# A planned GNN stack: batch-norm aggregation moved to GpSimd, a doubled recurrent state, and 67 single-pass state products

## The chip, the cores and the metric
The kernel runs on one core of one Trainium2 chip. The metric is the device time of one execution in microseconds (us), the median of several runs.

## The reference
The input `x` holds 32 batches of 512 tokens by 128 features, and `adj` is one 512 x 512 matrix that all batches share. Four layers follow, and each adds its result to `x`. Each starts from `h = relu(layernorm(x))`.

```python
# layer 0: graph convolution
A = adj + I;  d = A.sum(-1) ** -0.5
x = x + ((d[:, None] * A * d[None, :]) @ h) @ W.T + b
# layer 1: gated recurrent network, five steps (in_matrix and out_matrix are both adj)
m = adj @ h;  av = concat(m, m);  u3 = h @ u3_w.T
z = sigmoid(av @ w3_w.T + u3);  r = sigmoid(av @ w4_w.T + u3)
hv = tanh(av @ w5_w.T + (r * h) @ u5_w.T)
h = (1 - z) * h + z * hv
# layers 2 and 3: graph attention, softmax over the neighbours of each token
```
Everything is float32.

## The kernel before
All work is put into a list of operations by `op(engine, cost, due, emit, r, w, delay)` (class `Plan`). Each operation has an engine, a planned duration, a due time, a function that emits its instructions, and the buffers that it reads and writes. `Plan.run` simulates the five engines with these costs and delays, picks for each free engine the ready operation that is due first, and takes a buffer from its pool when an operation first needs one. The order found in this way is the order in which each engine's instructions are issued; each engine then executes in that order. `NUDGES` is a list of seeds that shift due times at random in stretches of the plan. So a changed cost, delay, buffer number or operation changes the order everywhere. Up to `LANES` = 6 batches are in the recurrent layer at once, one begun about every five planning slots.

A 128 x 512 product with float32 accuracy is made in one of two ways. One is a plain FP32 matmul (`weigh`, L807). The other takes three single passes (`one_pass`, L810; L691 for products with the adjacency matrix): `operands` (L664, L665, L667) makes three rounded tiles `upper`, `lower` and `across` with one ACT and two DVE operations; the passes of `upper` and `lower` add into a PSUM bank, ACT scales the bank by SPLIT + 1 (`rescale`, L673), and the pass of `across` is added.

`ggnn` normalizes a batch, brings it into feature order in `hT`, and calls `step` five times. A step has a product with `adj` (`in_three`), the gate r, the gate z in the same bank, and the candidate. In the steps of `STATE_GATES` the product with u3 takes three passes (`parts` of `by_m`), in the others an FP32 matmul. After r the bank is scaled back by 1/(SPLIT + 1), because z adds two unscaled passes first. Three DVE operations (L858, L859, L861) make the new state. `shuttle` carries the state back to token order by a DVE transpose (L642) into `sq` and five DMAs.

`norm_relu` makes the layernorm: `norm_stats` has four `bn_stats` (L553) and four `bn_aggr` (L557) on DVE. GpSimd then takes four operations on 128 x 4: add eps (L565), the power -0.5 (L566), the negated mean (L567), and its product with `rstd` (L570). Four ACT operations (L572) apply scale, offset and relu. `gcn` calls it for layer 0, `ggnn` for layer 1, and `gat` for the attention layers of batches 0 to 27 (the last four use `center_relu`). `add_onto` (L636) adds a result to `x` by a DMA that GpSimd issues, so these transfers and the small operations share one queue.

Of the kernel before, what the change touches and what calls it, by code (L numbers as in the profile page):

```python
# [24 lines left out]
FAR0 = 2  # L25
IDLE_FROM = 1342
# [3 lines left out]
STATE_GATES = {(b, s) for b in range(2, 32) for s in (2, 3) if s == 2 or b % 2}  # L30

NUDGES = (
    647971, 907480, 641022, 815328, 59938, 583104, 493449, 610727, 19299, 304899, 627144, 635903, 69303, 408061,
    213735, 192787, 7302, 58637, 834115, 963636, 6410, 705202, 955061, 53160, 882452, 878871, 458378, 231573,
    440371, 124696, 831158, 659333, 156550, 375431, 144007, 229366, 92171, 712320, 383813, 271697, 742240,
    798210, 397175, 163443, 123863, 724213, 516264, 896604, 122936, 743614, 457019, 570185, 62661, 920948,
    442263, 711198, 25011, 31858, 120261, 992683, 84663, 643357, 45247, 844390, 187975, 852865, 391757, 659128,
    736213, 659734, 397346, 484557, 410316, 685524, 527983, 521839, 433865, 543542, 868384, 394072, 205808,
    803310, 720274, 491124, 788541, 970038, 794737, 126558, 819621, 549318, 737826, 829243, 433351, 616176,
    868933, 314847, 688289, 939737, 907635, 853367, 672087, 953482, 982700, 636640, 260426, 745621, 974814,  # L40
    394689, 394423, 913904, 563868, 809734, 586161, 212429, 918084, 35227, 367565, 563487, 894884, 927872,
    820562, 407961, 31584, 797859, 266733, 239356, 49239, 168566, 825959, 690462, 633213, 766471, 952403,
    408935, 497281, 589831, 985192, 831666, 253050, 326020, 481827, 642272, 794393, 288155, 810682, 987219,
    726505, 745342, 441796, 26158, 800211, 187528, 795534, 149175, 951249, 42293, 197549, 962585, 253163,
    193842, 380099, 269941, 798210, 328761, 3598, 288464, 573452, 270841, 123133, 696935, 118976, 888464,
    549179, 731891, 706853, 313783, 900776, 668175, 816491, 294510, 923659, 444695, 534341, 679525, 202474,
    575303, 728118, 586387, 249556, 511121, 99992, 373622, 338542, 275589, 302881, 192606, 296189, 6121, 900716,
    93206, 158600, 419776, 382555, 10260, 855575, 704212, 698851, 696052, 457683, 55138, 404164, 139732, 866775,
    158170, 353170, 522421, 782841, 883529, 937879, 284896, 89904, 707913, 653847, 899032, 941515, 846706,
    471855, 178908, 722182, 666466, 211415, 810021, 295037, 269035, 402549, 983916, 571726, 473540, 395183,  # L50
    828707, 575084, 168839, 283291, 285134, 921509, 310987, 390552, 988218, 707221, 197452, 843224, 366926,
    884427, 545850, 986879, 832460, 861905, 777944, 317120, 973125, 261515, 931720, 503469, 106085, 519250,
    799711, 171717, 223192, 984270, 900296, 444443, 363172, 878758, 209540, 540746, 177829, 80204, 926590,
    322517, 646401, 549673, 224793, 442843, 438276, 448009, 366213, 419202, 112410, 62545, 971608, 549811,
    277513, 626388, 256930, 747343, 895280, 67763, 895530, 719737, 906641, 169362, 565633, 657856, 621526,
    269556, 28511, 630184, 65022, 38094, 940486, 350670, 532843, 24899, 947205, 540231, 223974, 479634, 329335,
    298114, 146538, 491725, 308524,
# [264 lines left out]
def gnn_stack(ctx: ExitStack, tc: tile.TileContext, a: dict, out: bass.AP):  # L322
# [13 lines left out]
    def flat(t):  # L336
# [8 lines left out]
        "sq": tiles(4, [P, Q, W * C], "sq"),  # L345
# [7 lines left out]
        "r": tiles(8, TOKENS, "r"),  # L353
# [13 lines left out]
        "ve": tiles(4, SMALL, "ve"),  # L367
        "rstd": tiles(8, SMALL, "rstd"),
# [28 lines left out]
    mhalf, eps, minus1 = (fixed(SMALL, k) for k in ("mhalf", "eps", "minus1"))  # L397
    warm = Val("r")
    op("POOL", 0.8, -1000, lambda: make_identity(nc, ident.t), w=[ident])
    for v, to in ((mhalf, -0.5), (eps, EPS), (minus1, -1.0)):  # L400
        op("POOL", 0.1, -999, lambda v=v, to=to: nc.gpsimd.memset(v.t, to), w=[v])
# [11 lines left out]
    for b in range(B):  # L413
        v = Val("x", C)
        op("SP", 0.5, -1002 if b == 0 else max(-995 + b, STEPS * b - 20) if b >= 8 else -995 + b,
           lambda v=v, b=b: nc.sync.dma_start(v.t, x[b].rearrange("(c p) d -> p c d", p=P)), w=[v], delay=(3.75, 5.2, 4.5, 5)[b] if b < 4 else 3)
        xs.append(v)
# [95 lines left out]
    def one(v):  # L513
        return [(v, 0, ident)]

    w0T = transposed(-11.7, one(w0), then=turned)
    gates = transposed((-9.5, -700, -700, -15.8), one(raw["u3"]), halves("w4"), halves("w3") + halves("w4", minus), halves("w5"), then=turned)
# [10 lines left out]
    u5T = transposed(-15.2, one(raw["u5"]), then=turned, by=0.5)  # L528
# [32 lines left out]
    def norm_relu(b, y, due, times=None):  # L561

        xb, off, rstd = xs[b], Val("off"), Val("rstd")
        mv = norm_stats(b, due)
        op("POOL", 0.5, due, lambda: nc.gpsimd.tensor_tensor(rstd.t, mv.t[:, :, 1], eps.t, ALU.add), r=[mv, eps], w=[rstd])  # L565
        op("POOL", 1.15, due, lambda: nc.gpsimd.tensor_tensor(rstd.t, rstd.t, mhalf.t, ALU.pow), r=[mhalf], w=[rstd])  # L566
        op("POOL", 0.42, due, lambda: nc.gpsimd.tensor_tensor(off.t, mv.t[:, :, 0], minus1.t, ALU.mult), r=[mv, minus1], w=[off])  # L567
        if times:
            op("DVE", 0.1, due, lambda: nc.vector.tensor_mul(rstd.t, rstd.t, times.t), r=[times], w=[rstd])
        op("POOL", 0.42, due, lambda: nc.gpsimd.tensor_tensor(off.t, off.t, rstd.t, ALU.mult), r=[rstd], w=[off], delay=2.6)  # L570
        for c in range(C):
            op("ACT", 0.385, due, lambda c=c: nc.scalar.activation(  # L572
                chunk(y, c), xb.t[:, c, :].rearrange("p (k j) -> p k j", k=Q) if y.kind == "h" else xb.t[:, c, :], AF.Relu, bias=off.t[:, c:c + 1], scale=rstd.t[:, c:c + 1]),
               r=[xb[c], off, rstd], w=[y[c * len(y.writers) // C]])
# [60 lines left out]
    def add_onto(x, what, reads, due):  # L635
        op("POOL", 1.0, due, lambda: nc.gpsimd.dma_start(x.t, what(), accum_op=ALU.add), r=reads, w=[x], delay=5.5)  # L636
# [147 lines left out]
    def ggnn(b, due):  # L784
        lane, h, hT = Val("lane"), Val("h" if b >= FAR0 else "y", C), Val("hT", Q)
        op("SP", 0.0, due - 3, lambda: None, r=[xs[b]], w=[lane], delay=0)
        op("SP", 0.0, due - 3, lambda: None, r=[lane], w=[h], delay=0)
        norm_relu(b, h, due - 2)
        if b >= FAR0:
            shuttle_first(h, hT, due - 2.5, due - 3)  # L790
        else:
            p = to_features(h, due - 2, hT)
            op("ACT", COPY, due - 2, lambda hT=hT: nc.scalar.copy(flat(hT.t), flat(p.t)), r=[p], w=[hT])
        for s in range(STEPS):
            now = due + LANES * s
            split = (b, s) not in WHOLE_GATES
            m = in_three(h, factors["adj"], now, split)
            if b == 4 and s == 0:
                op("SP", 0.0, now, lambda: None, r=[m[0] if split else m], w=[third], delay=0)
            h, hT = step(b, s, m, hT, now, lane)  # L800

    def step(b, s, m, hT, due, lane):
# [9 lines left out]
        def by_m(p, i, at, start, more=None, parts=None):  # L812
# [24 lines left out]
            op("PE", 2 * len(sums) * MR, at, first_two, r=[*of_gates[:2], *(v for _, three in sums for v in three[:2])], w=[p])  # L837
            rescale(p, at - 5)
            op("PE", len(sums) * MR + (MM if more else 0), at, third_one, r=[of_gates[2], *(three[2] for _, three in sums), *rest], w=[p])
# [9 lines left out]
        if split:  # L849
            rescale(gate, due - 5, 1 / (SPLIT + 1))  # L850
        by_m(gate, 2, due + 0.3, False)
        op("ACT", A, due - 5, lambda: nc.scalar.activation(flat(z.t), flat(gate.t), AF.Tanh, bias=gate_b["w3"].t, scale=0.5),
           r=[gate, gate_b["w3"]], w=[z])
        hv, new = Val("r"), Val("hT")
# [3 lines left out]
        op("DVE", V, due - 5, lambda: nc.vector.tensor_sub(flat(hv.t), flat(hv.t), flat(hT.t)), r=[hT], w=[hv])  # L858
        op("DVE", V, due - 5, lambda: nc.vector.scalar_tensor_tensor(flat(hv.t), flat(z.t), 1.0, flat(hv.t), op0=ALU.add, op1=ALU.mult),  # L859
           r=[z], w=[hv])  # L860
        op("DVE", V, due - 5, lambda: nc.vector.scalar_tensor_tensor(flat(new.t), flat(hv.t), 0.5, flat(hT.t), op0=ALU.mult, op1=ALU.add),  # L861
           r=[hv, hT], w=[new])
# [3 lines left out]
        if not EARLY <= due < STEPS * B:  # L866
            p = to_features(new, due + 2, *([] if last else [h]))
            if last:
                op("DVE", V, due + 2, lambda: nc.vector.tensor_add(flat(x.t), flat(x.t), flat(p.t)), r=[p, lane], w=[x])
# [5 lines left out]
        if last:  # L875
            mine = Val("y", 2)
            op("ACT", COPY, due + 2, lambda: nc.scalar.copy(
                mine.t.rearrange("p c (k j) -> p c k j", k=Q), h.t.rearrange("p k (c j) -> p c k j", c=C)), r=[h], w=[mine])
# [217 lines left out]
```

## Time and profile before

| what | us |
|---|---|
| median of 3 runs (1497.68 to 1499.28) | 1498.44 |
| the profiled execution | 1498.66 |
| its span, first to last instruction | 1496.7 |
| TensorE matmuls busy | 1486.3 |
| VectorE busy | 1408.1 |
| ScalarE busy | 1332.4 |
| GpSimd busy | 445.6 |

The span is shorter than the execution's time by 2.0 us, which lie around it. Engines run beside each other. PE is TensorE, PEld its weight loads, DVE VectorE, ACT ScalarE, POOL GpSimd, SP the queue that issues most DMAs. L with a number is a line of the kernel. A busy time is a union of instruction spans; successive instructions of one engine overlap a little in the trace, so distances between starts are also used.

### The profile page before, as it was taken

To read this page: it belongs to the slowest core of one execution; us is meant where nothing else is said; L and a number is where in the kernel's file an instruction comes from. 1 tells how busy PE (TensorE), PEld (TensorE's weight loads), DVE (VectorE), ACT (ScalarE), POOL (GpSimd) and SP (SyncE) were. 2 spreads that over 40 slices of the span, in tenths; PEclk is the share of its full clock that TensorE was granted. 3 is DMA by queue.
4 is the path that set the end of the run, shared out by engine and by line. 5 is a ranking of instruction groups with operands and counts; after the bars stand their busy time and mean duration, and the time that the engine had idled before them with its cause. 6 is when DMAs were issued, how large, how long until landed. Compare 5 with 4: busy or idle time off the path is not lost.

```text
span 1496.7 us, 25563 instructions
## 1 busy us (share of the span) xinstructions
PE 1486.3 (99%) x7464; PEld 1168.4 (78%) x7464; DVE 1408.1 (94%) x3323; ACT 1332.4 (89%) x2994; POOL 445.6 (30%) x636
## 2 busy tenths in 40 slices
PE   9999999999999999999999999999999999999999
PEld 7777777777777778777778777777777787777888
DVE  8989998999998998999999999999899999999898
ACT  6988998998989899989899989899889889989875
POOL 5411322222254223332323322333332214202321
PEclk9999999999999999999999999999999999999999
DMA  3345555645767567666665667666566565653233
GB/s 106 60 100 144 101 127 117 164 120 127 173 132 154 135 149 162 141 142 144 145 153 130 149 142 163 141 148 139 129 149 158 134 152 117 152 147 75 71 73 78
DMA packets 307499, 196.09 MB, mean 131 GB/s; under 512 B 87872, under 2 KB 259232, under 8 KB 307360
## 3 DMA queue, kind: packets, MB, share of 16 engines
q1 hardware_dynamic: 276160, 157.24, 40.8%
q0 software_dynamic: 30912, 36.71, 16.1%
q8 instruction: 59, 0.97, 0.3%
q14 instruction: 80, 0.66, 0.2%
q10 hardware_dynamic: 288, 0.52, 0.1%
HBM read 87.30 MB, written 70.37 MB: 105 GB/s over the span
## 4 chain that ended last, share of the span: by engine, by line
PE 54%; DVE 5%; ACT 4%; DMA 2%; issue 1%; SPq 1%; POOL 0%; DVEq 0%; ACTq 0%; POOLq 0%
PE bank L691 18%; PE bank L810 14%; PE bank L807 9%; PE bank L1001 8%; PE bank L932 3%; PE bank L987 1%; ACT bank L673 1%; DVE e L975 1%; PE bank L769 1%; DVE lower L665 1%; DVE across L667 1%; DMA far<-sq 1%; ACT upper L664 1%; DMA adjT<-y 1%; DVE sq L642 0%
## 5 line engine op out<-in xcount | busy, mean ns | idle before, releaser
L673 ACT ACTIVATE bank<-bank 128x512 f32<-128x512 f32 x820 | 466.4, 599 | 48.8 <-PE bank L691 35.4
L667 DVE SCALAR_TENSOR_TENSOR across<-lower,upper 128x512 fp32r<-128x512 f32 x391 | 260.2, 675 | 2.4 <-DVE lower L665 0.5
L810 PE MATMUL bank<-upper,gates 128*128 128x512 f32 x519 | 240.2, 463 | 0.1
L1001 PEld LDWEIGHTS bank<-h_gat,e 128*128 128x128 f32 x1792 | 220.3, 191 | 20.9 <-issue 12.0
L810 PE MATMUL bank<-across,gates 128*128 128x512 f32 x519 | 227.5, 466 | 1.0 <-ACT bank L673 0.9
L1001 PE MATMUL bank<-h_gat,e 128*128 128x129 f32 x1792 | 222.8, 275 | 0.0
L810 PE MATMUL bank<-lower,gates 128*128 128x512 f32 x519 | 204.9, 395 | 0.3 <-DVE lower L665 0.2
L691 PE MATMUL bank<-adj,across 128*128 128x512 f32 x640 | 188.3, 419 | 0.1
L691 PE MATMUL bank<-adj,upper 128*128 128x512 f32 x640 | 187.3, 414 | 0.0
L691 PE MATMUL bank<-adj,lower 128*128 128x512 f32 x640 | 175.4, 396 | 0.0
L636 POOL DMA_DIRECT2D x<-y x80 | 73.7, 928 | 315.4 <-ACT y L778 82.2
L565 POOL TENSOR_TENSOR rstd<-mv,eps 128x4 f32<-128x4 f32 x119 | 55.9, 470 | 371.4 <-DVE mv L557 363.0
L807 PE MATMUL bank<-r,wT 128*128 128x512 f32 x320 | 163.6, 593 | 2.0 <-DVE r L847 2.0
L975 DVE SCALAR_TENSOR_TENSOR e<-row,h_gat,maskT 128x512 f32<-128x512 f32 x224 | 156.9, 738 | 0.0
L566 POOL TENSOR_TENSOR rstd<-rstd,mhalf 128x4 f32<-128x4 f32 x119 | 150.4, 1264 | 1.5
L691 PEld LDWEIGHTS bank<-adj,across 128*128 128x128 f32 x640 | 117.5, 188 | 42.4 <-issue 12.5
L691 PEld LDWEIGHTS bank<-adj,upper 128*128 128x128 f32 x640 | 118.2, 188 | 37.0 <-issue 12.2
L691 PEld LDWEIGHTS bank<-adj,lower 128*128 128x128 f32 x640 | 120.4, 188 | 28.6 <-DVE lower L665 0.4
L810 PEld LDWEIGHTS bank<-across,gates 128*128 128x128 f32 x519 | 96.6, 188 | 49.1 <-ACT bank L673 20.3
L810 PEld LDWEIGHTS bank<-upper,gates 128*128 128x128 f32 x519 | 97.9, 189 | 37.9 <-issue 13.2
L845 ACT ACTIVATE r<-bank,gate_bw 128x512 f32<-128x512 f32 x160 | 111.1, 696 | 15.7 <-PE bank L807 15.4
L810 PEld LDWEIGHTS bank<-lower,gates 128*128 128x128 f32 x519 | 98.0, 189 | 32.7 <-issue 14.6
(153 smaller groups left out, 3073.1 us busy)
## 6 DMA issues: line engine op xcount, KB each, us to landing
far<-sq SPq DMA_DIRECT2D x936, 64.0 KB
h<-far SPq DMA_DIRECT2D x148, 256.0 KB
x<-y POOLq DMA_DIRECT2D x80, 256.0 KB, 4.3
sq<-far SPq DMA_DIRECT2D x56, 256.0 KB
row<-line SPq DMA_DIRECT2D x56, 256.0 KB
adjT<-y POOLq DMA_DIRECT2D x32, 256.0 KB, 4.2
hT<-far SPq DMA_DIRECT2D x120, 64.0 KB
x<-in_x_dram SPq DMA_DIRECT2D x24, 256.0 KB
```

The costliest lines, as they stand in the source:

```text
L565: op("POOL", 0.5, due, lambda: nc.gpsimd.tensor_tensor(rstd.t, mv.t[:, :, 1], eps.t, ALU.add), r=[mv, eps], w=[rstd])
L566: op("POOL", 1.15, due, lambda: nc.gpsimd.tensor_tensor(rstd.t, rstd.t, mhalf.t, ALU.pow), r=[mhalf], w=[rstd])
L636: op("POOL", 1.0, due, lambda: nc.gpsimd.dma_start(x.t, what(), accum_op=ALU.add), r=reads, w=[x], delay=5.5)
L667: op("DVE", V, due - 5, lambda: nc.vector.scalar_tensor_tensor(flat(across.t), flat(lower.t).bitcast(F32), -SPLIT, flat(upper.t).bitcast(F ...
L673: op("ACT", COPY, due, lambda: nc.scalar.mul(flat(p.t), flat(p.t), by), w=[p])
L691: nc.tensor.matmul(flat(p.t), left.t[:, c, :], right.t[:, c, :], start=first and c == 0, stop=c == C - 1, skip_group_check=True)
L807: nc.tensor.matmul(flat(p.t), (of or gates).t[:, i, :], flat(moving.t), start=start, stop=True, skip_group_check=True)
L810: nc.tensor.matmul(flat(p.t), of.t[:, i, :], flat(moving.t), start=start, stop=True, skip_group_check=True)
L845: op("ACT", A, due - 5, lambda: nc.scalar.activation(flat(r.t), flat(gate.t), AF.Tanh, bias=gate_b["w4"].t, scale=0.5), r=[gate, gate_b["w ...
L932: nc.tensor.matmul(qt()[:, c, :D + 3], gT.t[:, 2 * a + c, :], w_aug[l].t, start=True, stop=True)
L975: op("DVE", 0.661, due + 3, lambda j=j: nc.vector.scalar_tensor_tensor(e.t[:, j, :], matrix(row), h.t[:, j, D + 1:D + 2], mask.t[:, j, :], ...
L1001: nc.tensor.matmul(pt()[:, c, :D + 1], e.t[:, j, i * P:(i + 1) * P], h.t[:, j, :D + 1], start=(j == 0), stop=(j == C - 1))
```

## The change
Five things are changed.

1. The state is kept doubled: the layernorm of layer 1 multiplies `rstd` by two, the transposed gate weights are halved and those of u5 quartered, and the last step's result is halved. The new state is made from `kept = (z - 1) * hT`, which does not read the candidate, and two more DVE operations.
2. The z product adds its `across` pass first (`back=True`), on the scaled bank; the bank is then scaled back once and the other two passes follow. The tanh of z takes the factor SPLIT + 1 in its scale. The separate scaling between r and z is gone.
3. From batch 4 (`AGGR`) on, `norm_relu` has no `bn_aggr`. GpSimd combines the two halves' means and variances of `bn_stats` itself, in ten operations on 128 x 4 (one of them on 128 x 8).
4. `STATE_GATES` holds 67 steps instead of 45.
5. The planned delays of the loads of `x` (3 to 8) and of `add_onto` (5.5 to 7) are longer, `sq` has three buffers instead of four, `r` nine instead of eight, and the seeds are others.

```diff
+AGGR = 4
-STATE_GATES = {(b, s) for b in range(2, 32) for s in (2, 3) if s == 2 or b % 2}
+STATE_GATES = {(b, s) for b in range(2, 32) for s in (1, 2, 3) if s > 1 or b % 4 == 1}
...
-        "sq": tiles(4, [P, Q, W * C], "sq"),
+        "sq": tiles(3, [P, Q, W * C], "sq"),
...
-        "r": tiles(8, TOKENS, "r"),
+        "r": tiles(9, TOKENS, "r"),
...
-w=[v], delay=(3.75, 5.2, 4.5, 5)[b] if b < 4 else 3)
+w=[v], delay=(3.75, 5.2, 4.5, 5)[b] if b < 4 else 8)
...
+        if b < AGGR:
...
+        else:
+            st, both, apart = Val("st", C), Val("both"), Val("apart")
+            scale = root2 if state else root
+            for c in range(C):
+                op("DVE", 0.196, due, lambda c=c: nc.vector.bn_stats(st.t[:, c, :], xb.t[:, c, :]), r=[xb[c]], w=[st[c]])
+            pool(0.42, lambda: apart.t, lambda: st.t[:, :, 1], lambda: st.t[:, :, 4], ALU.subtract, [st], [apart])
+            pool(0.42, lambda: both.t, lambda: st.t[:, :, 1:3], lambda: st.t[:, :, 4:6], ALU.add, [st], [both])
+            pool(0.42, lambda: apart.t, lambda: apart.t, lambda: apart.t, ALU.mult, [], [apart])
+            pool(0.42, lambda: apart.t, lambda: apart.t, lambda: c32.t, ALU.mult, [c32], [apart])
+            pool(0.42, lambda: apart.t, lambda: apart.t, lambda: eps128.t, ALU.add, [eps128], [apart])
+            pool(0.42, lambda: rstd.t, lambda: apart.t, lambda: both.t[:, :, 1], ALU.add, [apart, both], [rstd])
+            pool(1.15, lambda: rstd.t, lambda: rstd.t, lambda: mhalf.t, ALU.pow, [mhalf], [rstd])
+            pool(0.42, lambda: rstd.t, lambda: rstd.t, lambda: scale.t, ALU.mult, [scale], [rstd])
+            pool(0.42, lambda: off.t, lambda: both.t[:, :, 0], lambda: nhalf.t, ALU.mult, [both, nhalf], [off])
...
-        op("POOL", 1.0, due, lambda: nc.gpsimd.dma_start(x.t, what(), accum_op=ALU.add), r=reads, w=[x], delay=5.5)
+        op("POOL", 1.0, due, lambda: nc.gpsimd.dma_start(x.t, what(), accum_op=ALU.add), r=reads, w=[x], delay=7)
...
+            if back:
+                op("PE", MR, at, third_one, r=one_of, w=[p])
+                rescale(p, at - 5, 1 / (SPLIT + 1))
+                op("PE", 2 * MR, at, first_two, r=two_of, w=[p])
+                return
...
-        if split:
-            rescale(gate, due - 5, 1 / (SPLIT + 1))
-        by_m(gate, 2, due + 0.3, False)
-        op("ACT", A, due - 5, lambda: nc.scalar.activation(flat(z.t), flat(gate.t), AF.Tanh, bias=gate_b["w3"].t, scale=0.5),
+        by_m(gate, 2, due + 0.3, False, back=True)
+        op("ACT", A, due - 5, lambda: nc.scalar.activation(
+            flat(z.t), flat(gate.t), AF.Tanh, bias=gate_b["w3"].t, scale=0.5 * (SPLIT + 1) if split else 0.5),
...
-        hv, new = Val("r"), Val("hT")
+        hv, kept, new = Val("r"), Val("r"), Val("hT")
+        op("DVE", V, due - 5, lambda: nc.vector.scalar_tensor_tensor(flat(kept.t), flat(z.t), -1.0, flat(hT.t), op0=ALU.add, op1=ALU.mult),
+           r=[z, hT], w=[kept])
...
-        op("DVE", V, due - 5, lambda: nc.vector.tensor_sub(flat(hv.t), flat(hv.t), flat(hT.t)), r=[hT], w=[hv])
...
-        op("DVE", V, due - 5, lambda: nc.vector.scalar_tensor_tensor(flat(new.t), flat(hv.t), 0.5, flat(hT.t), op0=ALU.mult, op1=ALU.add),
-           r=[hv, hT], w=[new])
+        op("DVE", V, due - 5, lambda: nc.vector.scalar_tensor_tensor(flat(new.t), flat(kept.t), -0.5, flat(hv.t), op0=ALU.mult, op1=ALU.add),
+           r=[hv, kept], w=[new])
```
The cut parts are the other norm branch (as before, with the product by two where the state is normed), the halved weights and results, six constants, and the seeds.

## Prediction
> **What bounds the kernel now.** I read the page's busy times and granted clock first, then the waits of TensorE, then the groups for the price of each operation, then the timeline for the true pace of the matmuls.
>
> ```profile
> PE 1486.3 (99%) x7464; PEld 1168.4 (78%) x7464; DVE 1408.1 (94%) x3323; ACT 1332.4 (89%) x2994; POOL 445.6 (30%) x636
> PEclk9999999999999999999999999999999999999999
> ```
> ```profile
> PE bank L807 <- DVE r L847: 2.0, 1, 2.0
> PE bank L409 <- DVE r L402: 1.1, 1, 1.1
> PE bank L810 <- ACT bank L673: 0.9, 3, 0.4
> ```
> TensorE is busy throughout at the full clock, and its three longest sorts of wait come to 4 us in 1496.7. A busy TensorE may still hide bubbles, so the pace of starts is the better measure:
>
> ```profile
> 800.26 0.80 PE L810 MATMUL bank<-across,gates 128*128 128x512 f32 x1
> 800.89 1.02 PE L807 MATMUL bank<-hT,wT 128*128 128x512 f32 x2
> 801.35 0.79 PE L810 MATMUL bank<-across,gates 128*128 128x512 f32 x1
> ...
> 809.23 0.39 PE L810 MATMUL bank<-upper,gates 128*128 128x512 f32 x1
> 809.46 0.40 PE L810 MATMUL bank<-lower,gates 128*128 128x512 f32 x1
> 809.70 0.40 PE L810 MATMUL bank<-upper,gates 128*128 128x512 f32 x1
> ```
> A single pass of 512 columns starts every 0.232 us. A single pass and an FP32 product together take 801.35 - 800.26 = 1.09, so the FP32 product (two records) takes 0.857. Short matmuls start every 0.1115 (sixteen in 1.78 in the chain). With the counts of the groups: 3813 single passes (519, 640 and 112, three times each) x 0.232 = 884.6; 281 FP32 products (320 + 230 + 12 records, halved) x 0.857 = 240.8; the other 3089 x 0.1115, with 5.0 more for L714's wider ones, = 349.4. Sum 1474.8. So 21.9 us of the span are not TensorE work: 1.1 before the first matmul, 3.5 behind the last, some 6 in the first 30 us while inputs land, and about 11 scattered. What shortens this kernel is TensorE work, or one of those 11.
>
> **TensorE work removed.** STATE_GATES grows from 45 to 67 steps (step 1 of seven batches and step 3 of the fifteen even ones). In each new one the u3 product goes from one FP32 product to three single passes: 0.857 - 3 x 0.232 = 0.161. Times 22: -3.5 us. Nothing else on TensorE changes in number; `back` only reorders the three passes of the z product. This lies wholly on the bound.
>
> **What the 22 cost elsewhere.** Each adds one ACT rounding and two DVE operations on 128x512:
>
> ```profile
> L664 ACT ACTIVATE upper<-hT 128x512 fp32r<-128x512 f32 x45 | 29.0, 646 | 1.9 <-DVE hT L861 1.8
> L665 DVE TENSOR_TENSOR lower<-hT,upper 128x512 fp32r<-128x512 f32 x45 | 30.2, 672 | 0.1
> L557 DVE BATCH_NORM_AGGREGATE mv<-st 128x2 f32<-128x6 f32 x480 | 43.9, 152 | 0.1
> L673 ACT ACTIVATE bank<-bank 128x512 f32<-128x512 f32 x820 | 466.4, 599 | 48.8 <-PE bank L691 35.4 <-PE bank L810 11.5
> ```
> ACT +22 x 0.64 = +14; DVE +44 x 0.675 = +30. In these steps the first two passes of the r product wait for ACT and DVE, and TensorE is in order behind them. The 45 steps that do so now show what that costs: ACT waits 1.9 us in all for hT, and no wait of a matmul for these tiles stands in the list: 0, at worst the 0.1 us hand-over in each, 2 us.
>
> **The step.** Before, the gate bank is scaled up, scaled back and scaled up again; afterwards the z product adds its third pass first and is scaled down once, the factor SPLIT + 1 going into the tanh's own scale. One L673 of 0.569 goes in each of 158 split steps: ACT -90. Net ACT 1332 - 90 + 14 = 1256 (84%). The doubled state keeps three DVE operations a step at the same 0.68 each, but `kept` needs only z, so two of them instead of three follow the candidate's tanh. Latency per step falls by one L673 and one DVE operation on different branches, some 0.6 to 0.8 us. With up to six batches interleaved this is hidden; it frees banks and lanes earlier. Its direct worth is put at nothing: the other batches' matmuls cover it, and without that cover it would be a gain of at most 0.7 at a step.
>
> **Norm statistics.** 28 first-layer, 28 second-layer and 48 attention norms of batches 4 to 27 or 31: 104 calls. Each loses four L557: 416 x 0.0915 = DVE -38. With the +30 DVE stays at 1400 (94%), so the DVE room freed is what pays for the new state products. Each call gains six GpSimd operations net (ten instead of four):
>
> ```profile
> L565 POOL TENSOR_TENSOR rstd<-mv,eps x119: 188/546/3109, 10.9 to 1429.8; 128x4 f32<-128x4 f32 x119
> L567 POOL TENSOR_TENSOR off<-mv,minus x119: 188/201/1232, 11.4 to 1430.0; 128x4 f32<-128x4 f32 x119
> ```
> The two groups' means are 470 and 403 and L570's is 551; I take 0.47: 624 x 0.47 = +293, POOL to about 740 (49%). One call's chain on POOL grows from 2.7 to some 5.5 us, behind nothing but an attention or lane start that the order places ahead. Today ACT's relu waits for that chain four times, 3.6 us in all. Unseen are the operations on strided `st` columns: between the free 0.19 and twice the mean, 0.94, so POOL gains 119 to 587 and ends between 38% and 69%; L565, which reads a strided column of `mv`, is nearest. In POOL's queue the accumulating DMAs (L636, 140 x 0.93 to 1.34) stand behind these operations and can start up to 2.8 us later; their planned landing is raised from 5.5 to 7. For TensorE both ends are 0 to +3 us, less nothing since a later norm can't help; I take +0.5. The four early state norms gain one POOL operation, and six constants some 0.1 each at the start, while POOL waits 6.3 us for DVE anyway (L589): 0.
>
> **A rule against this.** The trace first: a POOL operation that starts while DVE runs an operation with two SBUF inputs takes 0.62 us (L565, 67 of 119), else 0.28; and consecutive two-input DVE operations start every 602 ns (median) with a POOL operation beside them (396 cases) and every 602 without (1094). The Trainium skill, SBUF — State Buffer, "Who interferes with whom", says that these two contend for an exclusive lock, and whichever starts first blocks the other for its whole instruction. By the rule taken both ways, the 624 new operations at their free 0.19 would hold DVE for up to 119 us (an estimate), more than its 89 us of idle time: the kernel would become DVE bound near 1530. By the trace only POOL pays. I take the trace.
>
> **Loads and buffers.** The one long TensorE wait in mid-kernel is this:
>
> ```profile
> 414.09 0.48 DVE L553 BATCH_NORM_STATS2 st<-x 128x6 f32<-128x128 f32 x2 [3.91 <-DMA x<-in_x_dram]
> 414.49 0.67 DVE L847 SCALAR_TENSOR_TENSOR r<-r,hT 128x512 f32<-128x512 f32 x1
> 415.22 1.13 PE L807 MATMUL bank<-r,wT 128*128 128x512 f32 x2 [2.04 <-DVE r L847]
> ```
> DVE stood 3.9 us at a bn_stats whose x had not landed, with L847 queued behind it. The change plans x's landing at 8 instead of 3 us, so the order puts these statistics later: -1.9. What is late next there is an ordinary ACT or DVE hand-over of 0.1 to 0.4. `sq` loses a buffer (4 to 3): 234 transposes, with DMAs that hold each for roughly 8 to 15 us, keep about 1.5 in use (an estimate), so 0, at worst a microsecond. `r` gains the buffer that `kept` needs: 0. Order and seeds are new throughout; the other 9 scattered us are redrawn, with ACT five points freer: between -4 and +5, taken as 0.
>
> **Sum.** -3.5 - 1.9 + 0.5 = -4.9 on the profiled execution's 1498.66 (span 1496.7 and 2.0 around it): 1493.8. The median shown is 1498.44, 0.2 lower: 1493.6.
>
> **The rivals.** *Gain swallowed by the new order (0.18).* The matmul saving is 0.24%, hardly more than this kernel's measurement can tell from no change (0.2%, 3.0 us). If the redrawn stalls grow by 2 to 8, the time lies between 1495.4 and 1501.4. For it: 63 small waits make up the scattered time, and nothing ties them to what is edited. Against: ACT is relieved of 76 us and the one long wait is addressed.
>
> *GpSimd too late (0.10, slower).* Place: the norm chain on POOL behind an accumulating DMA that itself waits, since POOL is in order and its L636 waits reach 23 us. A late `off` holds ACT's relu, on an in-order ACT, and then every rescale behind it. Price: each such hold over the cover stops TensorE like the 2.0 us above. Four more of them (8 us) undo the 4.9 and pass +3, so it decides from there; six to eight give 1505 to 1510. For: POOL rises to half, and the chain doubles. Against: 3.6 us of such waits now.
>
> *ACT relief reaches TensorE (0.07).* If late rescales are behind most scattered stalls, another 6 go: 1486 to 1489. For: TensorE's weight loads wait 24.9 us for L673. Against: only 0.9 of it reached the matmuls.
>
> That the change does less than it says would show as a wrong count; 22 is exact from the two sets, so this has no share.
>
> **The numbers.** Likeliest (0.65): 1489 to 1495.4, at 1493.6. With the rivals: faster 0.72 (by over 0.2%), same 0.18, slower 0.10. The range 1488.3 to 1500.5 leaves out the slower case, the top of the swallowed one and most of the ACT relief.
>
> **What would show it.** FP32 u3 records 230 to 186; L810 passes 519 to 541 of each sort; the rescale group 820 to 662; L557 480 to 64; POOL near 740, ACT near 1256, DVE near 1400. The starts' pace must stay 0.232, and the work sum fall to 1471.3; span less this sum must be about 20.5. It is wrong if POOL `off` holds ACT for more than some 20 us, if two-input DVE operations take over 620 ns start to start, or if TensorE's waits beyond the first 30 us exceed those now.

## The result and the profile after

The changed kernel takes 1487.47 us (median of 4 runs, 1487.39 to 1488.39), beside 1498.74 for the kernel before on the same chip. The ratio is 0.9931, with a 95% interval of 0.9918 to 0.9943, so the gain is 10.3 us (8.5 to 12.3). The prediction said 4.9 less and named 1488.3 as the low end of its range. The median lies 0.8 us under that; the ratio, taken on the 1498.44 that the prediction started from, gives 1488.1.

The page of the changed kernel, its span and busy times:

```profile
span 1485.6 us, 25858 instructions
PE 1478.1 (99%) x7481; PEld 1171.1 (79%) x7481; DVE 1406.2 (95%) x2951; ACT 1271.5 (86%) x2858; POOL 662.5 (45%) x1270
```

The moves are as forecast in sign: ACT lost 61 us, GpSimd gained 217, DVE stayed. TensorE is still busy for 99%, which tells nothing of where 11 us went. The counts of its groups tell more. These are from the groups by line (the passes of the gate products, the FP32 products, the rescale):

```profile
L832 PE MATMUL bank<-upper,gates 128*128 128x512 f32 x541 | 257.2, 475 | 0.0
L829 PE MATMUL bank<-hT,wT 128*128 128x512 f32 x186 | 94.9, 592 | 0.0
L695 ACT ACTIVATE bank<-bank 128x512 f32<-128x512 f32 x662 | 381.1, 598 | 92.4 <-PE bank L713 56.8 <-PE bank L832 33.9
```

541, 186 and 662 are the forecast counts. With the prices of the prediction, TensorE's work is now 3879 x 0.232 + 259 x 0.857 + 3084 x 0.1115 + 5.0 = 1470.8 us, 4.0 less than before (0.5 of it are five short matmuls that this trace does not show). So the span's 11.1 us divide into 4.0 of work and 7.1 of time in which TensorE does not work: 21.9 before, 14.8 after (some 20.5 were forecast). The first matmul starts at 1.06 us in both, and the last ends 3.5 us ahead of the span's end in both; the 7.1 lie between.

Two waits tell part of it. First TensorE's own longest, after:

```profile
PE bank L411 <- DVE r L404: 1.1, 1, 1.1
PE bank L1017 <- DVE e L1005: 0.9, 2, 0.6
PE bank L455 <- DMA e<-in_adj_dram: 0.6, 1, 0.6
```

The wait of 2.0 us for L847 is gone, and what is left is start and tail. Second, DVE's groups of bn_stats, before and then after (the last column is idle time ahead of them):

```profile
L553 DVE BATCH_NORM_STATS2 st<-x 128x6 f32<-128x128 f32 x352 | 83.0, 276 | 16.0 <-DMA x<-in_x_dram 15.3 <-DMA x<-y 0.7
```
```profile
L580 DVE BATCH_NORM_STATS2 st<-x 128x6 f32<-128x128 f32 x288 | 67.9, 279 | 0.0
L580 DVE BATCH_NORM_STATS2 st<-adjT 128x6 f32<-128x128 f32 x128 | 30.2, 277 | 0.0
L555 DVE BATCH_NORM_STATS2 st<-x 128x6 f32<-128x128 f32 x64 | 15.0, 280 | 3.8 <-DMA x<-in_x_dram 3.8
```

Before, DVE lost 15.3 us to loads of x that had not landed, in nine waits. The first of them, 4.1 us, lies at the start of the kernel and is still there (3.8, L555 serves batches 0 to 3). The other eight, 11.2 us, are gone.

By stretches (the first columns are the stretch and TensorE's busy time with its matmuls), the kernel before and the one after:

```profile
400.00:500.00 100.00, 97.96 (x511) 77.95 (x510) 90.24 (x223) 87.89 (x204) 42.87 (x55) 1.00 0.69 152
600.00:700.00 100.00, 99.55 (x476) 77.10 (x475) 95.98 (x228) 90.94 (x205) 30.78 (x45) 1.00 0.63 141
```
```profile
400.00:500.00 100.00, 100.00 (x504) 79.39 (x504) 94.93 (x187) 87.60 (x199) 50.71 (x95) 1.00 0.64 142
600.00:700.00 100.00, 100.00 (x491) 78.50 (x491) 93.77 (x186) 88.15 (x198) 54.09 (x101) 1.00 0.64 142
```

The clock is full in all of them, and GpSimd's rise is visible beside a TensorE that shows as busy throughout.

### The profile page after: what moved, and what is told of

Read it like the earlier page. It is cut to its first block, busy times and chain, and to the rows that moved or that the text cites. A ratio compares the mean times of both kernels' runs of the same rounds, so it can differ in the third digit from the quotient of the medians.

```text
span 1485.6 us, 25858 instructions
## 1 busy us (share of the span) xinstructions
PE 1478.1 (99%) x7481; PEld 1171.1 (79%) x7481; DVE 1406.2 (95%) x2951; ACT 1271.5 (86%) x2858; POOL 662.5 (45%) x1270
## 4 chain that ended last, share of the span: by engine, by line
PE 97%; DVE 1%; ACT 0%; DMA 0%; issue 0%; ACTq 0%; DVEq 0%
PE bank L713 35%; PE bank L832 26%; PE bank L829 15%; PE bank L1031 13%; PE bank L962 4%; PE bank L791 2%; PE bank L1017 2%; PE bank L736 1%; PE bank L653 0%; DVE e L1005 0%; DMA e<-in_adj_dram 0%; PE bank L507 0%; PE bank L992 0%; DVE st L630 0%; PE bank L455 0%
## 5 line engine op out<-in xcount | busy, mean ns | idle before, releaser
L695 ACT ACTIVATE bank<-bank 128x512 f32<-128x512 f32 x662 | 381.1, 598 | 92.4 <-PE bank L713 56.8
L689 DVE SCALAR_TENSOR_TENSOR across<-lower,upper 128x512 fp32r<-128x512 f32 x413 | 276.5, 678 | 2.2
L832 PE MATMUL bank<-upper,gates 128*128 128x512 f32 x541 | 257.2, 475 | 0.0
L832 PE MATMUL bank<-across,gates 128*128 128x512 f32 x541 | 218.3, 445 | 0.1
L832 PE MATMUL bank<-lower,gates 128*128 128x512 f32 x541 | 214.1, 396 | 0.0
L713 PE MATMUL bank<-adj,across 128*128 128x512 f32 x640 | 183.8, 411 | 0.0
L568 POOL TENSOR_TENSOR apart<-st 128x4 f32<-128x4 f32 x104 | 53.7, 517 | 218.1 <-DVE st L580 216.1
L713 PEld LDWEIGHTS bank<-adj,upper 128*128 128x128 f32 x640 | 117.8, 188 | 34.7 <-issue 10.3
L832 PEld LDWEIGHTS bank<-upper,gates 128*128 128x128 f32 x541 | 102.0, 188 | 42.5 <-issue 14.6
L874 ACT ACTIVATE r<-bank,gate_bw 128x512 f32<-128x512 f32 x160 | 111.4, 699 | 24.1 <-PE bank L829 21.4
L832 PEld LDWEIGHTS bank<-lower,gates 128*128 128x128 f32 x541 | 102.1, 189 | 37.8 <-issue 19.1
L568 POOL TENSOR_TENSOR rstd<-rstd,mhalf 128x4 f32<-128x4 f32 x104 | 128.1, 1232 | 5.1
```

Source lines behind the costliest of these rows:

```text
L568: op("POOL", cost, due, lambda: nc.gpsimd.tensor_tensor(to(), one(), other(), how), r=r, w=w)
L695: op("ACT", COPY, due, lambda: nc.scalar.mul(flat(p.t), flat(p.t), by), w=[p])
L713: nc.tensor.matmul(flat(p.t), left.t[:, c, :], right.t[:, c, :], start=first and c == 0, stop=c == C - 1, skip_group_check=True)
L832: nc.tensor.matmul(flat(p.t), of.t[:, i, :], flat(moving.t), start=start, stop=True, skip_group_check=True)
L874: op("ACT", A, due - 5, lambda: nc.scalar.activation(flat(r.t), flat(gate.t), AF.Tanh, bias=gate_b["w4"].t, scale=0.5), r=[gate, gate_b["w ...
```

## Experiments

Three theories were to be told apart. A: ACT, relieved of 158 operations, keeps the planned hand-overs. B: loads of x are planned to land later, so DVE no longer stands at a bn_stats with other work queued behind it. C: the order that the new seeds make has fewer holes, whatever the operations are.

Times are medians; each ratio is to the kernel before on the same chip, whose median was 1497.3 to 1497.7 beside these runs. Differences from the changed kernel are differences of ratios, times 1498.4.

| kernel | us | ratio (95%) |
|---|---|---|
| a_act | 1540.39 | 1.0288 (1.0273 to 1.0304) |
| a_fp32 | 1494.43 | 0.9980 (0.9973 to 0.9988) |
| a_dve | 1543.06 | 1.0307 (1.0289 to 1.0324) |
| a_pool | 1532.06 | 1.0230 (1.0215 to 1.0246) |
| b_noz | 1496.12 | 0.9994 (0.9987 to 1.0000) |
| b_nox | 1493.15 | 0.9971 (0.9960 to 0.9982) |
| b_noz_nox | 1493.17 | 0.9968 (0.9956 to 0.9980) |
| a_noseed | 1501.75 | 1.0024 (1.0013 to 1.0035) |
| p_ctl | 1496.26 | 0.9987 (0.9979 to 0.9995) |
| p_act | 1495.63 | 0.9988 (0.9981 to 0.9994) |
| p_dve | 1493.01 | 0.9978 (0.9970 to 0.9985) |
| p_d3 | 1499.58 | 1.0011 (1.0002 to 1.0020) |

**Work put back behind the planner's back.** In the first four the operations that the planner sees are those of the changed kernel, so the order of every engine stays; only what an operation emits is altered.

```diff
 # a_act
-        op("ACT", COPY, due, lambda: nc.scalar.mul(flat(p.t), flat(p.t), by), w=[p])
+        def scaled():
+            nc.scalar.mul(flat(p.t), flat(p.t), by)
+            if twice:
+                nc.scalar.mul(flat(p.t), flat(p.t), 1.0)
+        op("ACT", COPY, due, scaled, w=[p])
...
-                rescale(p, at - 5, 1 / (SPLIT + 1))
+                rescale(p, at - 5, 1 / (SPLIT + 1), twice=True)
```


> The changed kernel, with each scaling-back of the z bank emitted twice (the second by 1.0), so that ACT again has the 158 operations that the change took from it; the planned order of every engine is kept. Theory A (ACT relief lets hand-overs keep the planned order): TensorE waits come back, 1491 to 1495. Theory B (the calmer planned delays of loads and accumulations did it): 1487 to 1489. Theory C (the new order itself has fewer holes, whatever the load of ACT): 1487 to 1489. ACT busy near 1360.

Measured 53.5 us more than the changed kernel, far outside all three theories. The page and one wait of a_act:

```profile
PE 1508.8 (98%) x7481; PEld 1164.4 (76%) x7481; DVE 1411.6 (92%) x2951; ACT 1352.1 (88%) x3016; POOL 650.0 (42%) x1270
PE bank L836 <- ACT bank L698: 12.0, 28, 1.2
```

ACT's load is then 88% of the span, less than its share before the change; it has room, and yet 81 us of ACT work cost 53 us. TensorE's matmuls are the same 1470.8 us of work. But the run does two things at once. The added scaling (L698, 0.58 us) stands between the third pass of a z product and its first two, so it also lengthens that hand-over in each of 158 steps, and TensorE waits 12.0 us for it directly. The 53 us are therefore no price of ACT's load alone; the run can't tell the two apart.

```diff
 # a_fp32: new_one is true in the 22 steps that STATE_GATES gained
-                for n, (k, (upper, lower, across)) in enumerate(sums):
+                for n, (k, (upper, lower, across)) in enumerate(sums[:1] if new_one else sums):
...
+                if new_one:
+                    weigh(p, 0, hT, of=gates)
```


> The changed kernel, with the u3 product of the 22 newly converted steps made by one FP32 matmul again; their rounded tiles are still made but not used for it, and the planned order is kept. If TensorE's work alone sets the time, 22 x 0.161 = 3.5 us come back: 1491.0. If the conversion is worth less because its matmuls stood beside waits, under 1490.

Measured 7.3 us more (4.5 to 10.5 from the ends of the two intervals). The counts give 1474.3 us of TensorE work, 3.5 more, which is the saving of the prediction; its span of 1492.7 leaves 18.4 without work instead of 14.8, the other 3.6. So the 22 conversions are worth their 3.5 us of matmuls, and taking them back without telling the planner costs about as much again in time without work.

```diff
 # a_dve
+            def stats(c):
+                nc.vector.bn_stats(st.t[:, c, :], xb.t[:, c, :])
+                nc.vector.bn_aggr(unread.t[:, c, :], st.t[:, c, :])
...
```


> The changed kernel with the 416 bn_aggr put back on DVE beside the GpSimd aggregation (their result is not read); order kept. DVE +25 to +38 us of 1406. If DVE's headroom carries the gain (a rival to theory A): 1492 or more. If DVE has enough left: 1487.5 to 1490.

Measured 56.3 us more. The page and two groups of a_dve:

```profile
PE 1504.5 (98%) x7481; PEld 1167.7 (76%) x7481; DVE 1473.2 (96%) x3367; ACT 1275.4 (83%) x2858; POOL 646.8 (42%) x1270
L582 DVE BATCH_NORM_AGGREGATE unread<-st 128x2 f32<-128x6 f32 x416 | 75.8, 182 | 14.4
```

The addition turned out larger than meant: DVE grew by 67 us, not 25 to 38, because here each aggregate directly follows the statistics that it reads (it starts 0.296 us after them, where another bn_stats starts after 0.193). So this is no exact undoing of the change, and its 56 us can't be read as the worth of the move to GpSimd.

```diff
 # a_pool
+            def twice():
+                nc.gpsimd.tensor_tensor(to(), one(), other(), how)
+                nc.gpsimd.tensor_tensor(unread.t, c32.t, eps128.t, ALU.add)
```


> The changed kernel with each of the nine GpSimd operations of the new norm followed by another one of 128x4 with two SBUF inputs into an unread tile; order kept. POOL +936 operations, some +350 to +440 us (70 to 75% busy). If only GpSimd pays for the shared port, two-input DVE operations still start every 602 ns. If DVE pays, up to 0.19 us for each: DVE busy +50 us or more and a time over 1500. The rival of a GpSimd that is too late: a doubled chain, 5 us more per norm, ends at 1495 to 1510; if the norms have enough lead, under 1490.

Measured 44.8 us more. The page, one group and one wait of a_pool:

```profile
PE 1494.9 (98%) x7481; PEld 1175.2 (77%) x7481; DVE 1409.9 (92%) x2951; ACT 1273.0 (83%) x2858; POOL 902.0 (59%) x2206
L571 POOL TENSOR_TENSOR unread<-c,eps 128x4 f32<-128x4 f32 x936 | 349.4, 373 | 0.0
ACT y L598 <- POOL off L596: 45.8, 29, 4.3
```

This is the slower rival of the prediction (GpSimd too late), at its place: ACT's relu waits for `off`, 45.8 us in 29 waits, where the same group of the changed kernel loses nothing:

```profile
L594 ACT ACTIVATE y<-x,off,rstd 128x128 f32<-128x128 f32 x260 | 115.9, 502 | 0.0
```

The run also settles who pays when GpSimd and DVE meet. Consecutive two-input DVE operations start every 602 to 603 ns (median) with a GpSimd operation beside them and every 602 without, in several hundred cases each, although GpSimd runs 2206 instructions instead of 1270. An added GpSimd operation that starts while DVE runs one with two SBUF inputs takes 0.66 us on average, and 2.5 at most; else it takes 0.22. Only GpSimd pays; the 45 us come from its lateness and not from DVE. A part of them is clock: in four stretches at long stalls of TensorE, 17 us in all, the granted clock is 0.5, which is worth 8.5 us at most.

**Work taken away from the kernel before.** Here too the order is kept. The first kernel leaves out a scaling and the second takes the statistics of another tile, so their values are not those of the reference; they are built for their time alone.

```diff
 # b_noz
         if split:
-            rescale(gate, due - 5, 1 / (SPLIT + 1))
+            op("ACT", COPY, due - 5, lambda: None, w=[gate])
 # b_nox, for the first layer from batch 8 on
...
-nc.vector.bn_stats(st.t[:, c, :], xb.t[:, c, :])
+nc.vector.bn_stats(st.t[:, c, :], (b0.t if loaded and b >= 8 else xb.t[:, c, :]))
...
```


> The kernel before, its order kept, with the scaling of the gate bank between r and z left out (so z is computed from an unscaled bank). ACT loses 158 operations that its plan still counts. Theory A (ACT's load held up TensorE in the kernel before): 3 to 6 us less, about 1493 to 1495 where before is 1498. Theory B (late loads of x held up DVE): no change. TensorE's work is the same in either.

> The kernel before, its order kept, with the first-layer statistics of batches 8 to 31 taken of a tile that is long there instead of the loaded x (DVE no longer stands at a bn_stats until x lands; 15.3 us of waits). Theory B: 2 us less at the wait of 415 us, up to 4 in all. Theory A: no change beyond 0.5.

> Both of these in the kernel before. If the two causes add and account for the change's gain beyond the 3.5 us of matmuls (7 to 8 us): 1490 to 1492. If the new order's own holes carry it (theory C): 1495 or more.

b_noz gains 0.9 us (0 to 1.9): theory A has next to nothing in the old order. b_nox gains 4.3 us (2.7 to 6.0), as theory B said, and the 2.0 us wait for L847 is gone from its list of TensorE's waits. Both together gain 4.8 (3.0 to 6.6), which can't be told from b_nox alone. In b_nox, this group of DVE stands for what was removed; it loses nothing ahead of it:

```profile
L553 DVE BATCH_NORM_STATS2 st<-b 128x6 f32<-128x128 f32 x96 | 23.1, 277 | 0.0
```

The traces also show where TensorE gets these 4.3 us. Take the start of each matmul, subtract the prediction's prices of all matmuls ahead of it, and what piles up is time lost for good. In 400 to 500 us and in 1050 to 1100 us, TensorE loses 4.7 us before, 0.4 in b_nox and nothing in the changed kernel. These are the stretches of DVE's longest waits for x: one of 3.9 us at 414, one of 1.8 at 470, and this one:

```profile
1050.86 0.68 DVE L553 BATCH_NORM_STATS2 st<-x 128x6 f32<-128x128 f32 x3 [3.43 <-DMA x<-in_x_dram]
```

Other stretches of 50 us differ by up to 0.7 us between the kernel before and b_nox, so the tenths mean little.

**The order.**

```diff
 # a_noseed
-NUDGES = (...)
+NUDGES = ()
```


> The changed kernel with an empty list of seeds: the planner's own order. Theory C: the seeds matter more than all else, 1500 to 1510. Theory A alone: within 5 us of 1487.

The planner's own order costs 13.9 us against the shipped list of seeds and is slower than the kernel before with its list. Operations, buffers and delays are the same as in the changed kernel.

**Undone in the plan, with a new order for each.** The last four have lists of seeds from the same search effort; one changes nothing else.

```diff
 # p_act
-        by_m(gate, 2, due + 0.3, False, back=True)
+        if split:
+            rescale(gate, due - 5, 1 / (SPLIT + 1))
+        by_m(gate, 2, due + 0.3, False)
... (the tanh of z takes scale=0.5 again)
 # p_dve
-AGGR = 4
+AGGR = 32
 # p_d3
-... if b < 4 else 8)
+... if b < 4 else 3)
-... w=[x], delay=7)
+... w=[x], delay=5.5)
```


> The changed kernel with seeds of its own: the list is emptied and filled by a new search of some 10,500 trials in the planner, the same effort as in the three kernels beside it. It is their control, and shows what another good order of the same operations costs: 1487 to 1492.

> The changed kernel with the old order of the z product in the plan: the bank is scaled back on its own, then up again (158 ACT operations more), and the plan knows it; seeds searched anew with the same effort. Theory A (ACT relief carries several us): 4 us or more above the control. Theory B (planned landings carry it) and the runs of the kernel before without these operations: within 2 us of the control.

> The changed kernel with bn_aggr on DVE for all batches (AGGR = 32) and four GpSimd operations a norm as before; planned, seeds searched anew with the same effort. If the move to GpSimd is what makes room for 67 state products: 4 us or more above the control, with waits for DVE. If DVE has the room anyway, or GpSimd's longer chain costs as much: within 2 us.

> The changed kernel with the planned delays of before (3 for a load of x, 5.5 for an accumulation); seeds searched anew with the same effort. Theory B: DVE stands at bn_stats for x again (10 us or more of such waits) and the time is 3 to 6 us above the control. Theory A: within 1 us of it.

The control missed its expectation: 1496.26, which is 8.4 us above the changed kernel with identical operations. Its span of 1494.6 holds 24.1 us without TensorE work, and its largest hole can be followed to its cause (lines of its timeline, then the stretch around them):

```profile
1364.92 4.38 POOL L543 TENSOR_TENSOR apart<-apart 128x4 f32<-128x4 f32 x1
1372.29 0.88 ACT L569 ACTIVATE y<-x,off,rstd 128x128 f32<-128x128 f32 x2 [3.94 <-POOL off L567]
1373.70 1.88 PE L688 MATMUL bank<-adj,across 128*128 128x512 f32 x4 [2.95 <-ACT bank L670]
1350.00:1400.00 50.00, 47.05 (x229) 36.43 (x228) 43.11 (x83) 40.73 (x91) 23.22 (x33) 0.97 0.29 61
```

Two norms run interleaved on GpSimd here, and three of their small operations take 3.19, 2.59 and, in the first line, 4.38 us, where the plan counts 0.42 each. ACT's relu stands 3.9 us for `off`, the rescale behind it is late, and TensorE stands 2.95 us; right behind the stall the granted clock is 0.5 for 3.4 us. TensorE loses 4.1 us here, about half of what the control lacks. So this part of the order's spread is the slower rival of the prediction, GpSimd too late, which the shipped order escapes.

p_act is level with the control (0.9988 beside 0.9987), although its page shows ACT at 1340.9 us instead of 1271.5. So 69 us of ACT work that the plan knows show no cost. But each of the two is one draw of the order, and p_act has such holes too (ACT waits 7.8 us for `off` in all, and TensorE loses 2.9 us at the longest of these waits), so a few us could hide in the draws. With b_noz, where the order is kept and 0.9 us is all that came of the relief, nothing is left that speaks for theory A.

p_dve has a lower median than the control by 3.3 us (1.3 by the ratios), with intervals that overlap. The planned bn_aggr make DVE 1429.3 us and leave GpSimd at 452.7:

```profile
PE 1482.0 (99%) x7482; PEld 1170.9 (78%) x7482; DVE 1429.3 (96%) x3367; ACT 1270.8 (85%) x2858; POOL 452.7 (30%) x674
```

So there is no sign that the move to GpSimd brings anything by itself: DVE had room for 67 converted products and the aggregates, and the control's 4.1 us hole stands at a moved norm. The shorter chain is not free of such waits either: in p_dve, ACT stands 2.6 us for `off` in all, and TensorE loses 1.0 us there.

p_d3 is 3.3 us above the control by medians, and the intervals are apart. The groups of bn_stats of later batches in p_d3, and then in p_ctl, each with the stretch of 400 to 500 us:

```profile
L555 DVE BATCH_NORM_STATS2 st<-x 128x6 f32<-128x128 f32 x288 | 68.8, 278 | 12.1 <-DMA x<-in_x_dram 10.7 <-DMA x<-y 1.4
400.00:500.00 100.00, 97.39 (x494) 76.89 (x493) 89.77 (x182) 84.80 (x194) 44.07 (x91) 0.98 0.67 149
```
```profile
L555 DVE BATCH_NORM_STATS2 st<-x 128x6 f32<-128x128 f32 x288 | 66.9, 278 | 0.0
400.00:500.00 100.00, 100.00 (x505) 79.06 (x504) 93.83 (x184) 88.71 (x203) 47.58 (x95) 1.00 0.66 147
```

The old delays bring back the waits for x, and TensorE loses 5.4 us in each of the two stretches with the longest of them (400 to 500 and 1100 to 1200), where the control loses next to nothing. That bears out the mechanism of theory B a second way. The 3.3 us are no measure of its size: some 3 us of these losses stand at other waits (a late `off`, another transfer), and the control has its own hole elsewhere. p_d3 restores both delays, so the accumulation's share in it stays open.

## Why the prediction was right and wrong

- **TensorE work, -3.5:** right. The trace has 4.0 less by count (0.5 of it missing short records), and a_fp32 has 3.5 more by count.
- **Loads of x, -1.9:** the mechanism was right and the size too small. I counted only the one wait that reached TensorE as a long one, and b_nox shows 4.3. The wait that was missed is DVE's 3.4 us at 1050.86: TensorE lost 1.7 us in the 50 us from 1050 on (0.3 in b_nox), in pieces too short for its list of waits. The wait at 470 adds some tenths.
- **The new order, taken as 0 within -4 to +5:** the range was too narrow. Orders of the same operations lie 8.4 us (p_ctl) and 13.9 us (a_noseed) above the shipped one, so the term can be as large as the whole gain. That it came out in favour was luck as far as the sum goes: with p_ctl's order the same change measures 1496.26. Of the 7.1 us of lost time that went, 4.7 lie in the stretches of the late loads; the other 2.4 are spread over the kernel, gains here and losses there, and I can only leave them to the order. No run gives the old operations an order as good as the new one.
- **The ACT relief, direct worth nothing:** right, and the rival that gave it another 6 us was wrong (b_noz, p_act), though the time came out near that rival's 1486 to 1489. A fitting time was no evidence for its mechanism.
- **GpSimd, +0.5 within 0 to +3:** in the shipped order no cost is visible, with no wait of the new relus for `off`. Its operations' durations add up to 729 us (474 before), but they overlap, and the busy time came to 662.5, not 740. The bound was wrong all the same: it reckoned with the mean of a small operation, 0.19 to 0.94 us, while p_ctl has three of 2.59 to 4.38 us in one place and loses 4.1 us there. Doubled without the plan's knowledge, the chain cost 44.8 us.
- **The norm move paying for the products:** not borne out. DVE's sum came out (1406 beside 1400), but p_dve did without the move and was no slower than the control.
- **The lock rule:** the trace decided rightly that only GpSimd pays. DVE's pace did not change when GpSimd's operations rose from 636 to 1270, and to 2206 in a_pool. What GpSimd pays was underrated: 0.62 us was the middle of a spread that reaches 4.9 us in the kernel before.
- **ACT near 1256:** it was 1271.5; the L695 that went were worth 85 us by union (466.4 to 381.1), not 90, and the new roundings took 15 (14 forecast); the other 9 I have not traced.

## What to carry to other kernels

Where the order of every engine is fixed before the run, an engine's idle share is no price list. In the plan, 69 us more on ACT showed no cost; behind the plan's back, 81 us at one hand-over of the step cost 53. Predict such a change in two terms: the change of the bound engine's work, which is reliable, and the order, whose spread has to be measured by running the same operations in another order before any few-us gain is put down to an edit. Then follow the largest holes of a bad order, since one can stand at something that the edit touched, as the late GpSimd chain here. Planned landing times of loads that are too early cost more than they seem to, since one late load holds an in-order engine and all that stands behind it.

## Hardware, unexpected

- An aggregate of batch statistics that directly follows the statistics it reads adds 0.161 us to DVE's busy time (67 us over 416 in a_dve), where four in a row after their statistics take 0.0915 each by union (43.9 over 480).
- A small GpSimd operation (128x4, inputs in SBUF) that starts while DVE runs one with two SBUF inputs mostly takes about 0.65 us, but some are passed over. In the changed kernel (without the powers), 48 of 303 take over 1 us where DVE's next operation has two SBUF inputs again, and none of 143 where it has not. Here one is passed over four times:

```profile
405.27 0.68 DVE L888 SCALAR_TENSOR_TENSOR r<-r,r 128x512 f32<-128x512 f32 x1
405.31 2.51 POOL L568 TENSOR_TENSOR apart<-apart 128x4 f32<-128x4 f32 x1
405.87 0.68 DVE L689 SCALAR_TENSOR_TENSOR across<-lower,upper 128x512 fp32r<-128x512 f32 x1
406.47 0.68 DVE L890 SCALAR_TENSOR_TENSOR hT<-r,r 128x512 f32<-128x512 f32 x1
407.07 0.68 DVE L687 TENSOR_TENSOR lower<-hT,upper 128x512 fp32r<-128x512 f32 x1
407.68 0.70 DVE L664 STREAM_TRANSPOSE sq<-hT 128x512 f32<-128x512 f32 x1
```

  It ends 0.14 us after the transpose has started. Of the 13 operations that take over 1.5 us, 12 end like this, 0.13 to 0.15 us after the start of the first following DVE instruction that has not two SBUF inputs (a transpose, statistics, or an operand in PSUM). The longest in p_ctl, 4.38 us, spans seven such DVE operations. DVE's pace stays at 602 ns.
